# A quarter of the scan output's addition moved from VectorE to TensorE and ScalarE

## The chip, the cores and the metric

The kernel runs on one core of one Trainium2 chip. A core has five engines with an instruction queue each: TensorE (PE in the profile, with its weight loads as PEld), VectorE (DVE), ScalarE (ACT), GpSimd (POOL) and SyncE (SP, which here only issues DMAs). The metric is the device time of one execution in microseconds (us).

## The reference, cut to what matters

Two layers follow each other on an image batch of shape (8, 128, 128, 128). Layer 0 is a linear attention. Layer 1 is a state-space layer with 256 inner channels: a projection, a depthwise convolution, and then a selective scan over the 16,384 pixels of an image in four directions. The four results are added, multiplied by a gate, normalised and projected. The change is in the scan, of which this is the part that matters:

```python
def step(xc, inp):
    dlt, dut, Bt, Ct = inp
    dA = jnp.exp(dlt[..., None] * A[:, None])
    xc = dA * xc + dut[..., None] * Bt[:, :, None, :]
    y = jnp.einsum('kbcn,kbn->kbc', xc, Ct)
    return (xc, y)
...
y = (y0 + y1 + y2 + y3).transpose(0, 2, 1)
```

The state size is 1, so per pixel and channel there is one state h, the output is h times a scalar C of the pixel, and the four directions' h*C are added into one y.

## The kernel before, in words

`tile_kernel` calls `layer0`, `layer1_front` and `layer1_scan` one after the other. All that changes is in `layer1_scan`. Its work is a list of 512 **units**: 8 output images, for each of them 4 slots (one scan direction of one image each), and in each slot 16 chunks of 1,024 pixels. Channels lie on the 128 partitions, in two halves `c` = 0, 1. The running sum `y` of the output image stays in SBUF. A slot's `place` is 0 to 3 in its image. At place 0 h*C is written to `y`; at places 1, 2 and 3 (384 units) it has to be added to what `y` holds. Half of the directions see the image transposed (`y_turned`), so that their chunk lies in `y` in runs of four neighbouring elements, 512 bytes apart.

The function `step(n)` issues the instructions of one step, and `in_order` makes every engine keep exactly the order in which they are issued. A step does the end of unit n-1, the scan of unit n and the preparation of unit n+1:

- `emit(n-1, half1)`, then `gather(n-1)` and `emit(n-1, 1-half1)`. A chunk has two halves of 512 pixels. For places 1 to 3, VectorE multiplies the first half by C and writes the product to PSUM (L1001 or L1005), and `gather` (L1013, VectorE) adds it from PSUM to `y`. The other half's product stays in `ubt` (L994, VectorE), and `add` (L1021, GpSimd, at the end of the step) adds that to `y`.
- `decay(n, c)` (L960, ScalarE): the exponential, written to PSUM over the `px` pair of banks that held delta. It comes with one activation-table load.
- `weigh(n, c)` (L963, GpSimd): delta times input, in place in `ubt`.
- `scan(n, c)` (L971 or L973, VectorE): the recurrence, one instruction for 1,024 pixels.
- `delta(n+1, c)` (L952, TensorE): two matmuls of 512 columns into a `px` pair of banks, and `soften(n+1, c)` (L956, ScalarE): softplus, with another table load.
- `spread(n, half)` (L979, TensorE): the row of C copied to all partitions in PSUM (`pc`).
- loads of later units on the SP queue (L934, L935, L941), and, while an image leaves (16 steps, those at place 0 of the next image), its gate, moments, projection and store.

[...] three `px` tiles of two banks each, and two single banks. The product of the first half goes into the `px` tile of `da[n, 1]`, whose content the scan has used up. `delta(n+1, 0)` writes that same tile next, so it waits until `gather(n-1)` has read it.

Of the kernel before, what the change touches and what calls it, by code (L numbers as in the profile page):

```python
# [8 lines left out]
F32 = mybir.dt.float32  # L9
BF16 = mybir.dt.bfloat16  # L10
AF = mybir.ActivationFunctionType
ALU = mybir.AluOpType
# [4 lines left out]
P = 128  # L17
B = 8
H = W = 128
L = H * W  # L20
NH, HD = 4, 32
NC2 = 2
R = 8
K = 4
GW = 4
GN = GW * H
# [740 lines left out]
def layer1_scan(ctx: ExitStack, tc, ubs, xps, zs, gs, dtw, dtb, a_log, gamma, beta, w_out, out):  # L767
# [15 lines left out]
    nc = tc.nc  # L783
    const = ctx.enter_context(tc.tile_pool(name="l2c", bufs=1))
    big = ctx.enter_context(tc.tile_pool(name="l2b", bufs=1))
    wp = ctx.enter_context(tc.tile_pool(name="l2w", bufs=3))
    sm = ctx.enter_context(tc.tile_pool(name="l2s", bufs=4))
# [16 lines left out]
    for dst, src, rows in ((wparts, dtw.rearrange("k r d -> r k d"), R), (bparts, dtb.rearrange("o (k d) -> o k d", d=D2), 1)):  # L804
        x = wp.tile([rows, K, D2], F32, name="w32", tag="sp", bufs=2)
        nc.sync.dma_start(x, src)
        q = wp.tile([rows, 3, K, D2], BF16, name="w16", tag="ub", bufs=4)
# [14 lines left out]
    for i in range(3):  # L822
        t = const.tile([P, CH], BF16, name=f"rows{i}")
# [3 lines left out]
    for i in range(3):  # L827
        t = const.tile([P, D2], BF16, name=f"dtw{i}")
        nc.gpsimd.memset(t, 0.0)
        dws.append(t)  # L830
    csel = const.tile([P, P], BF16, name="csel")
    nc.gpsimd.memset(csel, 0.0)
    nc.gpsimd.memset(csel[96:99, :], 1.0)


    wg = const.tile([P, NC2, P], F32, name="wg")
# [4 lines left out]
    means = wp.tile([P, P], F32, name="means", tag="r", bufs=2)  # L841
    nc.vector.memset(means, 1.0 / (NC2 * P))

    mean = const.tile([P, 32], F32, name="mean2")
    nc.vector.memset(mean, 0.0)
    nc.vector.memset(mean[:, 0:1], 1.0 / (NC2 * P))
    sel = const.tile([P, NC2, 2], F32, name="sel")
    nc.vector.memset(sel, 0.0)
    for j in range(2):
# [64 lines left out]
    units = []  # L914
    for o in range(B):
        for s in ([3, 0, 1, 2] if o % 4 < 2 else [1, 2, 3, 0]):
            sl = Slot(len(units) // NCH, o, s)
            units += [(sl, i) for i in range(NCH)]

    ubt, sp, da = {}, {}, {}  # L920
# [6 lines left out]
    def load_rows(n):  # L927
        sl, i = units[n]
        m = sl.at(i)
        rw = rws[n % 3]  # L930
        md = NCH - 1 - m if sl.dt_turned_back else m
        src = xps[sl.dt_image, sl.dt_order].rearrange("j r l -> (j r) l")
        for j in range(3):
            nc.sync.dma_start(rw[3 * NR * j : 3 * NR * j + 3 * NR, :], src[:, md * CH : md * CH + CH])  # L934
        nc.sync.dma_start(rw[96:99, :], xps[sl.b, sl.order, :, R + 1, m * CH : m * CH + CH])  # L935
# [18 lines left out]
    def soften(n, c):  # L954
        sp[n, c] = t = wp.tile([P, CH], F32, name="sp", tag="sp", bufs=2)
        nc.scalar.activation(t, da[n, c], AF.Softplus)  # L956

    def decay(n, c):
        sl, i = units[n]
        nc.scalar.activation(da[n, c], sp[n, c], AF.Exp, scale=sa[:, sl.s, c : c + 1])  # L960

    def weigh(n, c):
        nc.gpsimd.tensor_tensor(ubt[n][:, c, :], ubt[n][:, c, :], sp.pop((n, c)), ALU.mult)  # L963
# [8 lines left out]
        else:  # L972
            nc.vector.tensor_tensor_scan(e, x, e, start, ALU.mult, ALU.add)  # L973

    cps, ts = {}, {}

    def spread(n, hf, tag):
        cps[n, hf] = p = pe.tile([P, 1, GN], F32, name="pc", tag=tag)
# [1 line left out]

    def emit(n, hf):

        sl, i = units[n]
        h = ubt[n][:, :, hf * 512 : hf * 512 + 512]
        c = cps.pop((n, hf)).to_broadcast([P, NC2, GN])
        if sl.place == 0:
            v = sl.y_at(i, hf)
            split = "p c (a b) -> p c a b"  # L990
            nc.vector.tensor_tensor(v, h.rearrange(split, b=H), c.rearrange(split, b=H), ALU.mult)
            return
        if hf != sl.first:
            nc.vector.tensor_tensor(h, h, c, ALU.mult)  # L994
            return
        p = da.pop((n, 1))
        if sl.y_turned:
            ts[n] = p.rearrange("p (c b a) -> p c b a", c=NC2, a=GW)
            t = p.rearrange("p (c b a) -> p c a b", c=NC2, a=GW)
            split = "p c (a b) -> p c a b"  # L1000
            nc.vector.tensor_tensor(t, h.rearrange(split, b=H), c.rearrange(split, b=H), ALU.mult)  # L1001
        else:
            t = p.rearrange("p (c q) -> p c q", c=NC2)
            ts[n] = t.rearrange("p c (a b) -> p c a b", b=H)
            nc.vector.tensor_tensor(t, h, c, ALU.mult)  # L1005

    def gather(n):

        sl, i = units[n]
        v = sl.y_at(i, sl.first)  # L1010
        if sl.y_turned:
            v = v.rearrange("p c a b -> p c b a")
        nc.vector.tensor_tensor(v, v, ts.pop(n), ALU.add)  # L1013

    def add(n):
# [8 lines left out]
    zt, rst, pts, mv = {}, {}, {}, {}  # L1024
# [8 lines left out]
    def fetch(o, m):  # L1033
        for hf in range(2):
            zt[m, hf] = z = wp.tile([P, NC2, GN], F32, name="z", bufs=6)
            p = mirrored(o, m, hf)
            nc.sync.dma_start(z, zs[o].rearrange("c p l -> p c l")[:, :, p * GN : p * GN + GN])

    def gate(o, m, hf, eng):
        z, ym = zt[m, hf], piece(m, hf)  # L1040
        eng.tensor_tensor(z, ym[:, :, ::-1] if o % 2 == 1 else ym, z, ALU.mult)

    def square(m, hf):
        nc.scalar.activation(piece(m, hf), zt[m, hf], AF.Square)  # L1044

    def moments(m):

        pm = pe.tile([P, GN], F32, name="pm", tag="pt")
        for c in range(NC2):
            for j in range(2):  # L1050
                for hf in range(2):
                    at = 32 * (2 * j + hf)
                    v = piece(m, hf) if j else zt[m, hf]
                    nc.tensor.matmul(pm[at : at + 32, :], mean, v[:, c, :], start=(c == 0), stop=(c == NC2 - 1))  # L1054
        pts[m, "rows"] = pm

    def keep(m):
        pm = pts[m, "rows"]
        pts[m, "rows"] = sr = wp.tile([P, GN], F32, name="sr", bufs=1)
        nc.scalar.copy(sr, pm)  # L1060
# [9 lines left out]
        nc.scalar.activation(t, pts[m][:, :, :, 0], AF.Square)  # L1070

    def variance(m):
        rst[m] = rstd = sm.tile([P, GW, NC2], F32, name="rstd")
        nc.vector.tensor_tensor(rstd, pts.pop(m)[:, :, :, 1], mv.pop(m), ALU.subtract)  # L1074

    def deviation(m):
        rstd = rst[m]
        nc.gpsimd.tensor_scalar(rstd, rstd, 0.0, EPS1, ALU.max, ALU.add)
        nc.gpsimd.tensor_tensor(rstd, rstd, half, ALU.pow)
# [22 lines left out]
    for o in range(B):  # L1102
        n = (o + 1) * K * NCH
        for j in range(NCH):
            e = o, NCH - 1 - j if o % 2 == 1 else j
# [11 lines left out]
    def step(n):  # L1117
        live = 0 <= n < N
        then = n + 1 < N
        before = 1 <= n <= N  # L1120
        now, last, soon, later = (leaving.get(n + i) for i in (0, -1, 1, 2))
        first = before and units[n - 1][0].place == 0
        if before:
            half1 = units[n - 1][0].first
            emit(n - 1, half1)
            if not first:
                gather(n - 1)
        if now and last:
            gate(*now, 1, nc.vector)
        if before:  # L1130
            emit(n - 1, 1 - half1)
        if n + 2 < N:
            load_rows(n + 2)
        if n in fetched:
            fetch(*fetched[n])
        if live:
            decay(n, 0)
        if now:
            square(now[1], 1)
        if live:  # L1140
            decay(n, 1)
            weigh(n, 0)
        if last:
            deviation(last[1])
        if live:
            weigh(n, 1)
        if now:
            moments(now[1])
        if live:
            scan(n, 0)  # L1150
            da.pop((n, 0))
        if last:
            for hf in range(2):
                store(*last, hf)
        if then:
            for c in range(NC2):
                delta(n + 1, c)
        if now:
            keep(now[1])
        if then:  # L1160
            soften(n + 1, 0)
        if now:
            to_tokens(now[1])
            square_mean(now[1])
        if then:
            soften(n + 1, 1)
        if live:
            scan(n, 1)
        if first:
            ubt.pop(n - 1)  # L1170
            if n + 3 < N:
                load(n + 3)
        if now:
            variance(now[1])
        if live:
            half1 = units[n][0].first
            spread(n, half1, "pc")
            spread(n, 1 - half1, "pt")
        if soon and now:
            gate(*soon, 0, nc.gpsimd)  # L1180
        elif soon:
            gate(*soon, 1, nc.gpsimd)
        elif later:
            gate(*later, 0, nc.gpsimd)
        if soon:
            square(soon[1], 0)
        if now:
            p = da.pop((n, 1)) if live else px.tile([P, CH], F32, name="px")
            for hf in range(2):
                project(now[1], hf, p[:, hf * 512 : hf * 512 + 512])  # L1190
        elif live and units[n][0].place == 0:
            da.pop((n, 1))
        if before and not first:
            add(n - 1)
            ubt.pop(n - 1)
        if n + 3 < N and not first:
            load(n + 3)
        if n in weighed:
            units[weighed[n]][0].weights()
        if n in summed:  # L1200
            add_d(*summed[n])
# [78 lines left out]
```

## Time and profile before

| what | value |
|---|---|
| median of 3 runs | 9476.79 us (9473.5 to 9477.35) |
| profiled execution: its time, its span | 9477.74 us, 9475.9 us |
| mean granted TensorE clock over the span | 0.792 |
| busy: DVE, POOL, ACT, PE, PEld | 8149.5, 7474.3, 7125.4, 6389.1, 3122.5 us |
| scans L971 and L973, 512 each | 1178.4 and 1176.9 us busy, 2332 ns each |
| `gather` L1013, 384 | 468.7 us busy, 1221 ns each |
| `add` L1021, 768 | 1155.3 us busy, 1550 ns each |

The page gives busy time per engine as a sum over three functions with different limits; the scan part fills roughly the second half of the span. A busy share close to one in a stage points at the engine that sets the time there, and the chain of waits says whether it really does.

### The profile page before, as it was taken

The page shows a single profiled execution, that of the slowest core. Times are in us where ns is not written, and L with a number is a line of the kernel's source. Part 1 is how long each engine was busy: PE and PEld are TensorE (multiplying, and loading weights), DVE is VectorE, ACT ScalarE, POOL GpSimd, SP SyncE. Part 2 cuts the span into 40 slices and gives each one's busy share as a digit, 9 for nine tenths or more (in the row PEclk, how much of TensorE's full clock was granted, in tenths as well). Part 3 has the DMA queues.
Part 4 walks back from the last instruction along what each step waited for, and adds up shares of the span by engine and source line. Part 5 has one row for each costly group of instructions (what it writes and reads, how often), then busy time and mean ns, then how long its engine had stood idle before and what let it go on. Part 6 is the DMA issues. An engine that isn't in the chain of part 4 may idle for free. (4 is left out here: it accounts for less than half of the span.)

```text
span 9475.9 us, 89695 instructions
## 1 busy us (share of the span) xinstructions
PE 6389.1 (67%) x24352; PEld 3122.5 (33%) x24352; DVE 8149.5 (86%) x8046; ACT 7125.4 (75%) x8034; POOL 7474.3 (79%) x4743
## 2 busy tenths in 40 slices
PE   8999999898989887788633644637345363543636
PEld 5555555564333332233200311304023040320403
DVE  6667765563999999999789999999999999999996
ACT  5556655567888887788678888888878888888884
POOL 3445544455789987788769999999999999999997
PEclk9999999999999998899855755758566585665857
DMA  2331233314598898999955958769586685967858
GB/s 92 134 134 71 106 134 132 133 63 152 180 230 244 231 231 229 233 232 224 226 158 171 273 154 228 223 181 264 158 238 203 190 256 166 247 187 201 248 163 214
DMA packets 1510245, 1784.08 MB, mean 188 GB/s; under 512 B 799444, under 2 KB 1025364, under 8 KB 1501552
## 3 DMA queue, kind: packets, MB, share of 16 engines
q1 hardware_dynamic: 1456496, 1577.01, 53.5%
q0 software_dynamic: 53248, 201.34, 11.4%
q8 instruction: 199, 3.26, 0.1%
q14 instruction: 302, 2.47, 0.1%
HBM read 1085.92 MB, written 692.12 MB: 188 GB/s over the span
## 5 line engine op out<-in xcount | busy, mean ns | idle before, releaser
L963 POOL TENSOR_TENSOR ubt<-ubt,sp 128x1024 f32<-128x1024 f32 x1024 | 2458.0, 2458 | 160.0 <-ACT sp L956 96.1
L952 PE MATMUL px<-rows,dtw 128*128 128x512 bf16 x2048 | 953.6, 565 | 2238.4 <-DVE y L1013 1069.2
L515 POOL TENSOR_TENSOR tap<-tap 128x1024 f32<-128x1024 f32 x512 | 1261.4, 2468 | 234.3 <-ACT tap L513 209.2
L523 DVE SCALAR_TENSOR_TENSOR acc<-xb,cw,acc 128x1024 f32<-128x1024 f32 x1024 | 1320.6, 1290 | 54.0 <-ACT xb L492 1.7
L956 ACT ACTIVATE sp<-px 128x1024 f32<-128x1024 f32 x1024 | 1046.2, 1024 | 418.1 <-PE px L952 351.0
L1021 POOL TENSOR_TENSOR y<-y,ubt 128x512 f32<-128x512 f32 x768 | 1155.3, 1550 | 146.0 <-DVE ubt L994 144.9
L505 PE MATMUL acc<-xi,wt 128*128 128x512 f32 x2048 | 1028.1, 648 | 314.3 <-ACT ures L530 314.3
L973 DVE TENSOR_TENSOR_SCAN ubt<-px,ubt 128x1024 f32<-128x1024 f32 x512 | 1176.9, 2332 | 27.4 <-POOL ubt L963 20.3
L971 DVE TENSOR_TENSOR_SCAN ubt<-px,ubt 128x1024 f32<-128x1024 f32 x512 | 1178.4, 2332 | 13.1 <-POOL ubt L963 6.0
L952 PEld LDWEIGHTS <-dtw 128*128 128x128 bf16 x2048 | 164.6, 109 | 3065.9 <-issue 869.7
L960 ACT ACTIVATE px<-sp,sa 128x1024 f32<-128x1024 f32 x1024 | 1110.1, 1109 | 6.1
L513 ACT ACTIVATE tap<-xb,cw 128x1024 f32<-128x1024 f32 x768 | 828.3, 1140 | 134.9 <-DVE acc L521 85.4
L282 POOL TENSOR_TENSOR q<-q,qs 128x512 f32<-128x512 f32 x256 | 271.7, 1061 | 698.2 <-DVE qs L281 698.2
L956 ACT ACT_TABLE_LOAD x512 | 656.9, 1283 | 169.6 <-PE px L952 146.9
L505 PEld LDWEIGHTS acc<-xi,wt 128*128 128x128 f32 x2048 | 398.1, 205 | 917.6 <-issue 497.1
L960 ACT ACT_TABLE_LOAD x512 | 656.9, 1283 | 9.0
L1086 PEld LDWEIGHTS px<-wg,z 128*128 128x128 f32 x4096 | 556.6, 219 | 117.9 <-issue 112.7
L979 PE MATMUL pc<-rows,csel 128*128 128x512 bf16 x1024 | 515.8, 584 | 81.3 <-DVE rstd L1074 77.5
L1086 PE MATMUL px<-wg,z 128*128 128x128 f32 x4096 | 556.7, 302 | 0.0
L478 PE MATMUL pxb<-xi,wi 128*128 128x512 f32 x1024 | 483.7, 595 | 10.1 <-DMA xi<-x 7.9
L1013 DVE TENSOR_TENSOR y<-y,px 128x1024 f32<-128x1024 f32 x384 | 468.7, 1221 | 14.4
L298 ACT ACTIVATE sq<-o 128x512 f32<-128x512 f32 x256 | 161.2, 630 | 420.1 <-DVE o L296 418.9
(160 smaller groups left out, 15379.7 us busy)
## 6 DMA issues: line engine op xcount, KB each, us to landing
ubt<-ubs SPq DMA_DIRECT2D x512, 1024.0 KB
zs<-z SPq DMA_DIRECT2D x512, 256.0 KB
ubs<-ures SPq DMA_DIRECT2D x256, 512.0 KB
ubs<-turned SPq DMA_DIRECT2D x256, 512.0 KB
z<-zs SPq DMA_DIRECT2D x256, 512.0 KB
y<-gs POOLq DMA_DIRECT2D x128, 1024.0 KB, 10.4
rows<-xps SPq DMA_DIRECT2D x1536, 60.0 KB
xi<-x SPq DMA_DIRECT2D x120, 576.0 KB
```

The lines of the kernel that those rows point to most:

```text
L505: nc.tensor.matmul(acc[:, s, :], wt[:, j, c, :], x, start=(j == 0), stop=(j == len(ON_PE) - 1))
L513: nc.scalar.activation(t, at(n, c, *d), AF.Copy, scale=cw[:, c, tap(*d) : tap(*d) + 1])
L515: nc.gpsimd.tensor_tensor(sums[n, c], sums[n, c], t, ALU.add)
L523: nc.vector.scalar_tensor_tensor(acc, at(n, c, *d), cw[:, c, tap(*d) : tap(*d) + 1], acc, ALU.mult, ALU.add)
L952: nc.tensor.matmul(p[:, hf * 512 : hf * 512 + 512], sl.dw[:, c * P : c * P + P], src, start=True, stop=True)
L956: nc.scalar.activation(t, da[n, c], AF.Softplus)
L960: nc.scalar.activation(da[n, c], sp[n, c], AF.Exp, scale=sa[:, sl.s, c : c + 1])
L963: nc.gpsimd.tensor_tensor(ubt[n][:, c, :], ubt[n][:, c, :], sp.pop((n, c)), ALU.mult)
L971: nc.vector.tensor_tensor_scan(e[:, ::-1], x[:, ::-1], e[:, ::-1], start, ALU.mult, ALU.add)
L973: nc.vector.tensor_tensor_scan(e, x, e, start, ALU.mult, ALU.add)
L1021: nc.gpsimd.tensor_tensor(v[:, c], v[:, c], h[:, c], ALU.add)
L1086: nc.tensor.matmul(po[:, w, :], z[:, c, w * H : w * H + H], wg[:, c, :], start=(c == 0), stop=(c == NC2 - 1))
```

## The change

The first half's product and addition are split into two quarters of a chunk. For one quarter, VectorE goes on as before: product to PSUM, `gather` adds it to `y`. For the other quarter, VectorE leaves the product in `ubt`, TensorE adds `y` and the product by multiplying both with a float32 identity matrix and accumulating in the second bank of the same `px` tile (`sum_first`, L1026), and ScalarE copies the sum to `y` (`keep_first`, L1032). "Quarter" is the half of the inner dimension, so in `y` the two quarters interleave. `emit_first` (L1013 and L1016 of the new numbering) issues the two products, `gather` is L1038, and the other half's product is L989. Two constant matrices become one column read with a stride of zero, one small buffer has three copies in place of four, and an identity of 128 x 128 is added.

```diff
-    csel = const.tile([P, P], BF16, name="csel")
+    csel = const.tile([P, 1], BF16, name="csel")
...
+    csel = csel.to_broadcast([P, P])
+    ident = const.tile([P, P], F32, name="ident2")
+    make_identity(nc, ident)
...
+    def emit_first(n):
...
+        p = da.pop((n, 1))
+        e = quarter(h, 1 - q)
+        nc.vector.tensor_tensor(e, e, quarter(c, 1 - q), ALU.mult)
+        ts[n], mine[n] = (piece_of(sl, p[:, j * GN : j * GN + GN]) for j in range(2))
+        t = ts[n].rearrange("p c b a -> p c a b") if sl.y_turned else ts[n]
+        nc.vector.tensor_tensor(t, quarter(h, q), quarter(c, q), ALU.mult)
+
+    def sum_first(n):
...
+        v = quarter(sl.y_at(i, sl.first), q)
+        xs = [contiguous(sl, x) for x in (v, quarter(hs(n, sl.first), q))]
+        for c in range(NC2):
+            for j, x in enumerate(xs):
+                nc.tensor.matmul(mine[n][:, c], ident, x[:, c], start=(j == 0), stop=(j == 1))
+
+    def keep_first(n):
...
+        v = contiguous(sl, quarter(sl.y_at(i, sl.first), q))
+        nc.scalar.copy(v, mine.pop(n))
 
     def gather(n):
 
         sl, i = units[n]
-        v = sl.y_at(i, sl.first)
-        if sl.y_turned:
-            v = v.rearrange("p c a b -> p c b a")
+        v = contiguous(sl, quarter(sl.y_at(i, sl.first), 0 if sl.back else 1))
         nc.vector.tensor_tensor(v, v, ts.pop(n), ALU.add)
...
-            emit(n - 1, half1)
-            if not first:
+            if first:
+                emit(n - 1, half1)
+            else:
+                emit_first(n - 1)
+                sum_first(n - 1)
                 gather(n - 1)
...
         if live:
             decay(n, 1)
+        if before and not first:
+            keep_first(n - 1)
+        if live:
             weigh(n, 0)
```

More of the change, by code (lines that the diff above doesn't have):

```diff
@@ L842, in layer1_scan @@
     nc.vector.memset(means, 1.0 / (NC2 * P))
-    mean = const.tile([P, 32], F32, name="mean2")
-    nc.vector.memset(mean, 0.0)
-    nc.vector.memset(mean[:, 0:1], 1.0 / (NC2 * P))
+    mean = const.tile([P, 1], F32, name="mean2")
+    nc.vector.memset(mean, 1.0 / (NC2 * P))
+    mean = mean.to_broadcast([P, 32])
     sel = const.tile([P, NC2, 2], F32, name="sel")
@@ L973, in scan @@
             nc.vector.tensor_tensor_scan(e, x, e, start, ALU.mult, ALU.add)
-    cps, ts = {}, {}
+    cps, ts, mine = {}, {}, {}
     def spread(n, hf, tag):
@@ L981, in emit @@
     def emit(n, hf):
+        h = hs(n, hf)
+        c = cps.pop((n, hf)).to_broadcast([P, NC2, GN]).rearrange("p c (a b) -> p c a b", b=H)
         sl, i = units[n]
[L986 to L992, printed above, removed]
@@ L993, in emit @@
-        if hf != sl.first:
-            nc.vector.tensor_tensor(h, h, c, ALU.mult)
-            return
-        p = da.pop((n, 1))
-        if sl.y_turned:
[L998 to L1005, printed above, removed]
+        nc.vector.tensor_tensor(sl.y_at(i, hf) if sl.place == 0 else h, h, c, ALU.mult)
@@ new lines, in hs, with quarter, contiguous, piece_of @@
+    def hs(n, hf):
+        return ubt[n][:, :, hf * 512 : hf * 512 + 512].rearrange("p c (a b) -> p c a b", b=H)
+    def quarter(v, last):
+        return v[:, :, :, H // 2 :] if last else v[:, :, :, : H // 2]
+    def contiguous(sl, v):
+        return v.rearrange("p c a b -> p c b a") if sl.y_turned else v
+    def piece_of(sl, bank):
+        if sl.y_turned:
+            return bank.rearrange("p (c b a) -> p c b a", c=NC2, a=GW)
+        return bank.rearrange("p (c a b) -> p c a b", c=NC2, a=GW)
@@ new lines, in emit_first @@
+    def emit_first(n):
+        sl, i = units[n]
+        hf, q = sl.first, 0 if sl.back else 1
+        h = hs(n, hf)
+        c = cps.pop((n, hf)).to_broadcast([P, NC2, GN]).rearrange("p c (a b) -> p c a b", b=H)
+        p = da.pop((n, 1))
+        e = quarter(h, 1 - q)
[3 more added lines that the diff above has]
+        nc.vector.tensor_tensor(t, quarter(h, q), quarter(c, q), ALU.mult)
@@ new lines, in sum_first @@
+    def sum_first(n):
+        sl, i = units[n]
+        q = 1 if sl.back else 0
+        v = quarter(sl.y_at(i, sl.first), q)
[4 more added lines that the diff above has]
+    def keep_first(n):
+        sl, i = units[n]
+        q = 1 if sl.back else 0
+        v = contiguous(sl, quarter(sl.y_at(i, sl.first), q))
+        nc.scalar.copy(v, mine.pop(n))
@@ L1007, in gather @@
     def gather(n):
         sl, i = units[n]
-        v = sl.y_at(i, sl.first)
-        if sl.y_turned:
-            v = v.rearrange("p c a b -> p c b a")
+        v = contiguous(sl, quarter(sl.y_at(i, sl.first), 0 if sl.back else 1))
         nc.vector.tensor_tensor(v, v, ts.pop(n), ALU.add)
@@ L1072, in variance @@
     def variance(m):
-        rst[m] = rstd = sm.tile([P, GW, NC2], F32, name="rstd")
+        rst[m] = rstd = sm.tile([P, GW, NC2], F32, name="rstd", bufs=3)
         nc.vector.tensor_tensor(rstd, pts.pop(m)[:, :, :, 1], mv.pop(m), ALU.subtract)
```

## Prediction

> **What bounds the kernel now.** I read the page's slices first, then the stages, then the chain and one step of the timeline. In the scan part (from slice 20 on) VectorE is at 9 tenths and TensorE's granted clock is near half. The stage view separates the two kinds of step:
>
> ```profile
> core 0: us, PE busy (x) PEld busy (x) DVE busy (x) ACT busy (x) POOL busy (x), PEclk, DMA share, GB/s
> 5294.00:5475.00 181.00, 143.47 (x986) 102.08 (x979) 170.98 (x219) 146.72 (x158) 164.94 (x89) 0.93 0.94 277
> 5481.00:5873.00 392.00, 141.16 (x298) 27.95 (x298) 383.33 (x239) 320.88 (x285) 373.57 (x201) 0.50 0.62 180
> ```
>
> The first row is 16 steps in which an image leaves, the second is steps of places 1 to 3, which the change touches. There VectorE is busy 98% of the time, GpSimd 95%, and the clock is 0.50 throughout. The chain of waits in that stretch lies on VectorE alone:
>
> ```profile
> 5602.41 1.24 DVE px L1001
> 5603.67 1.10 DVE y L1013
> 5604.81 1.01 DVE ubt L994
> 5605.82 0.12 issue
> 5605.94 4.47 DVE ubt L971 x2
> 5610.46 0.04 issue
> ```
>
> One step is product, gather, other product, two scans. The starts of those scans lie 8.22 us apart in nearly every step of places 1 to 3. Taken apart by starts: 1.26 (product, which gather needs), 1.14 (gather), 1.13 (other product), 4.69 (two scans and the way back). TensorE and ScalarE wait for VectorE:
>
> ```profile
> 5604.95 1.04 PE L952 MATMUL px<-rows,dtw 128*128 128x512 bf16 x2 [2.94 <-DVE y L1013]
> 5606.09 1.28 ACT L956 ACT_TABLE_LOAD   x1 [0.32 <-PE px L952]
> ```
>
> Delta's matmul starts 0.06 us after gather's end (5603.67 + 1.22), and 0.10 us after its own end ScalarE goes on: the two hand-over prices used below.
>
> [...] The wait priced below comes from how the program guards its buffers.
>
> **The change part by part, per step of places 1 to 3 (384 units).**
>
> *VectorE's work.* Removed: half of gather. Added: the product becomes two instructions of 512 elements. The nearest row is L272, 128x512:
>
> ```profile
> L272 DVE TENSOR_TENSOR q<-pq,qm 128x512 f32<-128x512 f32 x256 | 177.2, 692 | 26.7 <-DVE qm L270 0.9
> L551 PE MATMUL pb<-xd,ident 128*128 128x512 f32 x512 | 240.8, 593 | 0.7 <-ACT xd L543 0.7
> L1060 ACT COPY sr<-pm 128x512 f32<-128x512 f32 x128 | 75.0, 586 | 209.0 <-PE pm L1054 209.0
> ```
>
> So 0.69 us each. A follower that needs nothing of the one before starts some 0.09 us before its end (1.13 against 1.22), hence 0.60 from start to start. If nothing else happened: 0.60 (first product) + 0.73 (second, then the dependent gather) + 0.60 (gather) + 1.13 + 4.69 = 7.75 instead of 8.22: a gain of 0.47 us.
>
> *TensorE's sum.* Four matmuls of 256 columns in float32. The trace records each float32 matmul as two passes. Their price in this clock comes from L1086, passes of 128 columns:
>
> ```profile
> 5322.34 3.73 PE L1086 MATMUL px<-wg,z 128*128 128x128 f32 x32
> 5336.14 6.07 PE L1086 MATMUL px<-wg,z 128*128 128x128 f32 x32
> 5313.80:5334.10 20.30, 13.61 (x107) 9.35 (x105) 18.02 (x26) 14.87 (x16) 20.08 (x11) 1.00 1.04 292
> 5334.30:5340.90 6.60, 6.57 (x30) 6.00 (x31) 5.91 (x6) 5.55 (x7) 5.12 (x5) 0.50 1.02 350
> ```
>
> The first group ran at full clock: (3.73 - 0.17 for the last to drain) / 32 = 0.11 us a pass. The second ran 4.86 us at half clock (until 5341.0) and 1.21 us at full. The fast part holds (1.21 - 0.17) / 0.11 = 9 passes, so 23 took 4.86 us: 0.21 each. A 256-column pass is then 0.22 us at full and 0.43 us at half clock, and the eight passes of the sum are 1.7 or 3.4 us, plus a drain of 0.2. That the stationary matrix is an identity makes it no cheaper: L551 multiplies with one and takes 593 ns for 512 columns at mostly full clock, as other float32 rows do (L1054: 628). Weight loads, 0.2 us in L505's and L1086's rows, lie beside such passes.
>
> *Where the sum lies.* This decides. In the changed kernel's built order, the first identity matmul waits for VectorE's **second** product (same `px` tile, though another bank), and in all 384 units gather waits for the **last** identity matmul. Gather writes one quarter of `y` while TensorE reads the other; they interleave, and the program guards the whole range. So the sum stands between second product and gather on the engine that bounds the step, and the other product and both scans queue behind gather. Nothing hides it. Per step at half clock:
>
> 0.60 (first product) + 0.69 (second, to its end) + 0.06 + 3.41 + 0.21 + 0.08 (hand-overs, sum, drain) + 0.60 (gather) + 1.13 + 4.69 = 11.47 us, **3.25 us more** than 8.22. At full clock 9.77, 1.55 more.
>
> *Which clock.* TensorE's step becomes 3.4 (sum) + 0.85 (delta 0), a pause, 0.85 + 0.86 (delta 1, spread), a pause. [...] I take 3.2.
>
> *ScalarE's copy.* 586 ns by L1060. It waits for gather and then for nothing: `decay(n, 1)` ends 3.4 us into the step, gather after 5.7. Delta 0, its table load and softplus stand behind it. After gather: copy 0.65, delta 0 1.1, table load 1.28, softplus 1.02, second softplus after scan 0's delta 1 (10.3 to 11.3), table load, exponentials done by 3.4 us into the next step, whose first scan starts at 6.8. Covered by the stalled VectorE. If the stall were gone it would not be: then decay 1, copy 0.53, delta 0 with hand-overs 1.2, table 1.28, two softplus 1.97, table 1.3, two exponentials 2.16 form a ring of 8.5 us, longer than 8.22.
>
> *GpSimd.* 7.9 us of work per step, starting later, still within 11.4. *DMA.* As many issues as before; loads of `ubt` also wait for TensorE's reads, done well before. *The constants and the buffer.* `csel` and `mean` as one column: same weight loads, TensorE has spare time there; the identity is built once. Nothing.
>
> *Sum.* 384 x 3.2 = 1,229 us on the profiled execution's 9477.74 gives 10,707; the median is 1 us lower. I round down to **10,700**, since in the steps at an image's end, 9.5 to 10.2 us long, a little of the stall may lie beside other waits.
>
> *Unknown.* In transposed slots the product is read by TensorE in steps of 512 bytes. [...] Here a ScalarE copy read that way (L617) took 1988 ns against 1007 (L487), 1.9 ns an element. At half clock a pass takes 1.7 ns a column anyway, so the least is nothing and my value is nothing; the most, twice the time for four of eight passes, is 1.7 us in 192 steps, 330 us. [...]
>
> **The rivals.**
> - *Fast clock.* If the longer sum lifts the clock for good, the step is 9.77: 384 x 1.55 = 595, some 10,070; half of the steps give 10,380. For it: the stages with an image leaving run at 0.93. Against it: the pauses above. 0.10.
> - *Strided reads at full price*: 11,030. 0.10.
> - *The wait costs nothing at run time*, as if the sum were done when gather comes. Then the ring over ScalarE decides: (8.5 - 8.22) x 384 = 107, about 9,585. 0.05.
> - *Faster.* The sum leaves VectorE's path and the fast clock takes 0.4 us off delta 0 in the ring (8.1). Then GpSimd at 7.95 or that ring bound the step, and 0.1 to 0.27 x 384 gives 9,375 to 9,440. It needs sum and hand-overs under 0.47 us of VectorE's time against 3.8 priced. 0.03.
> - *Nothing in effect*, sums cancelling: 0.02, within 0.2%, which is about what a measurement of this kernel can tell from no change.
> - The main case: 0.70, own range 10,550 to 10,850.
>
> **How the numbers follow.** The forecast is the main case. The range 10,370 to 10,930 takes in its errors, the nearer half of the fast-clock case and most of the strided one. Chances: faster 0.03, same 0.02, slower 0.95.
>
> **What would show it.** Gather's idle time before it, released by PE L1026, of 3.5 us or more per step; VectorE's share in these stretches down from 98% to about 70%; scan starts 11.4 us apart; L1026 eight passes of 0.43; clock mostly 0.5 with single fast windows. I am wrong if gather follows the second product at once, if the clock stays at 1 through the sum, or if transposed slots have longer steps than the others by over 0.3 us.

## The result and the profile after

The changed kernel takes 10644.99 us (median of 6 runs, 10636.52 to 10652.03) against 9476.14 us before (median of 6): a ratio of 1.1235, 95% interval 1.1221 to 1.125. It is slower by 1,169 us; the forecast was 10,700, with a range of 10,370 to 10,930. The profiled execution of the changed kernel took 10636.52 us, 1,158.8 more than the profiled one of before.

VectorE's busy tenths and the granted clock in 40 slices, from the page of the kernel before and then from that of the changed kernel:

```profile
DVE  6667765563999999999789999999999999999996
PEclk9999999999999998899855755758566585665857
...
DVE  6666655739999999977687686786776866867765
PEclk9999999999999889975686685675766856867768
```

In the right half, the stage of the scans, VectorE now stands at 6 to 8 tenths, where it was at 9 almost throughout, and the clock moves mostly between 0.5 and 0.8. The group of gather before, then those of gather, of the sum's matmuls and of the copy in the changed kernel (engine, tiles, count, busy us, mean ns, then the idle time just before them and who ended it):

```profile
L1013 DVE TENSOR_TENSOR y<-y,px 128x1024 f32<-128x1024 f32 x384 | 468.7, 1221 | 14.4
...
L1038 DVE TENSOR_TENSOR y<-y,px 128x512 f32<-128x512 f32 x384 | 264.1, 688 | 1368.8 <-PE px L1026 1368.8
...
L1026 PE MATMUL px<-y,ident 128*128 128x256 f32 x1536 | 787.5, 611 | 528.0 <-DVE px L1016 528.0
...
L1026 PE MATMUL px<-ubt,ident 128*128 128x256 f32 x1536 | 764.3, 591 | 0.0
...
L1032 ACT COPY y<-px 128x512 f32<-128x512 f32 x384 | 224.1, 584 | 513.3 <-DVE y L1038 513.3
```

VectorE sat idle before gather for 1368.8 us, and all of it ended with TensorE's sum: 3.56 us for each of 384 gathers, where before it was 14.4 us in all. VectorE's busy time fell from 8149.5 to 7960.6 us, 0.49 us for each gather. The two together, 1,354 - 189 = 1,165 us, are the loss within 7 us.

The chain of waits in one step of place 1 (start, us, what):

```profile
5695.85 0.69 DVE ubt L1013
5696.54 0.62 DVE px L1016
5697.15 0.04 issue
5697.20 3.80 PE px L1026 x8
...
5701.02 0.07 DVE y L1038
...
5701.62 1.22 DVE ubt L989
5702.84 4.51 DVE ubt L974 x2
...
5707.45 0.69 DVE ubt L1013
```

Where gather stood in the chain before with 1.10 us, there are now 3.80 us of TensorE's sum, and then 0.62 us until the other product starts (5701.00 to 5701.62), in which the shorter gather lies. The step is 11.60 us (5695.85 to 5707.45), where it was 8.22.

By place, the mean from scan start to scan start, taken from the traces (images 2 to 8), with all such steps of the kernel summed:

| place | before, us | after, us | all steps, before and after, us |
|---|---|---|---|
| 0 | 11.22 | 11.05 | 1371, 1351 |
| 1 | 8.36 | 11.71 | 1067, 1497 |
| 2 | 8.22 | 11.42 | 1052, 1462 |
| 3 | 8.31 | 10.93 | 1056, 1387 |

Places 1 to 3 give 430 + 410 + 331 = 1,171, place 0 gives back 20, and the first scan starts 7 us later: within 2 us the 1,158.8 of the profiled executions. That place 3 loses less is the clock, below.

### The profile page after: what moved, and what is told of

Same layout as the page of the kernel before. It is cut to its first block, busy times and chain, and to the rows that moved or that the text cites. A ratio compares the mean times of both kernels' runs of the same rounds, so it can differ in the third digit from the quotient of the medians.

```text
span 10634.7 us, 97031 instructions
## 1 busy us (share of the span) xinstructions
PE 7607.5 (72%) x27424; PEld 4006.0 (38%) x27424; DVE 7960.6 (75%) x8429; ACT 7320.6 (69%) x8418; POOL 7468.7 (70%) x4745
## 4 chain that ended last, share of the span: by engine, by line
DVE 21%; ACT 13%; PE 11%; DMA 4%; issue 4%; SPq 0%; DVEq 0%; ACTq 0%; POOL 0%
DVE ubt L974 7%; DVE ubt L976 7%; PE px L1026 6%; ACT px L963 4%; DVE ubt L989 4%; ACT sp L959 3%; ACT L963 3%; PE px L955 2%; DMA out<-r 2%; DVE r L1117 2%; ACT L959 2%; PE px L1111 2%; DVE ubt L1013 1%; DVE px L1016 1%; DMA ubt<-ubs 1%
## 5 line engine op out<-in xcount | busy, mean ns | idle before, releaser
L966 POOL TENSOR_TENSOR ubt<-ubt,sp 128x1024 f32<-128x1024 f32 x1024 | 2411.4, 2372 | 649.4 <-ACT sp L959 576.3
L955 PE MATMUL px<-rows,dtw 128*128 128x512 bf16 x2048 | 870.3, 543 | 1666.6 <-DVE ubt L976 675.6
L1038 DVE TENSOR_TENSOR y<-y,px 128x512 f32<-128x512 f32 x384 | 264.1, 688 | 1368.8 <-PE px L1026 1368.8
L1026 PE MATMUL px<-y,ident 128*128 128x256 f32 x1536 | 787.5, 611 | 528.0 <-DVE px L1016 528.0
L959 ACT ACTIVATE sp<-px 128x1024 f32<-128x1024 f32 x1024 | 1023.4, 1023 | 123.2 <-POOL y L1046 63.3
L955 PEld LDWEIGHTS <-dtw 128*128 128x128 bf16 x2048 | 209.9, 116 | 2283.2 <-issue 1118.1
L1026 PE MATMUL px<-ubt,ident 128*128 128x256 f32 x1536 | 764.3, 591 | 0.0
L1026 PEld LDWEIGHTS px<-y,ident 128*128 128x128 f32 x1536 | 399.8, 288 | 956.6 <-DVE px L1016 814.8
L1032 ACT COPY y<-px 128x512 f32<-128x512 f32 x384 | 224.1, 584 | 513.3 <-DVE y L1038 513.3
```

The costliest lines, as they stand in the source:

```text
L955: nc.tensor.matmul(p[:, hf * 512 : hf * 512 + 512], sl.dw[:, c * P : c * P + P], src, start=True, stop=True)
L1026: nc.tensor.matmul(mine[n][:, c], ident, x[:, c], start=(j == 0), stop=(j == 1))
```

## The experiments

The theory after the result: VectorE's step waits for TensorE's sum, and the clock sets how long. The rivals: the copy on ScalarE with all that stands behind it, or the added work itself wherever VectorE stands. A "ring" in the expectations is a chain of waits that comes back to the same instruction one or two steps later, and so sets the least time of a step. All lines of code are changes to the changed kernel, and times stand against its 10,645 us and against about 9,470 of the kernel before. half_sum, no_copy, gather_first and delta_twice are one execution each; vector_only and late_sum are medians of 4, own_bank of 9.

**half_sum: half of the sum.**

```diff
-        for c in range(NC2):
+        for c in range(1):
             for j, x in enumerate(xs):
                 nc.tensor.matmul(mine[n][:, c], ident, x[:, c], start=(j == 0), stop=(j == 1))
```

> The changed kernel, but TensorE sums only channel half c = 0 of the quarter (four passes in place of eight); for c = 1 the sum is left out, so that quarter of y is not valid. Theory (gather waits for TensorE's sum, and VectorE's whole step waits behind it): the stall before gather falls from 3.57 us on average by four passes, some 1.7 us at half clock, less where the clock is already fast: steps of places 1 to 3 of 9.6 to 10.0 us and a total of 9,980 to 10,120 us. Rival (the time goes to ScalarE's copy and what stands behind it, or to the hand-overs between engines, whatever the size of the sum): over 10,450 us.

Measured: 10097.38 us; steps of 9.9 to 10.0 us. Its gather and sum, from the groups:

```profile
L1026 PE MATMUL px<-y,ident 128*128 128x256 f32 x768 | 443.2, 678 | 398.5 <-DVE px L1016 398.5
L1038 DVE TENSOR_TENSOR y<-y,px 128x512 f32<-128x512 f32 x384 | 264.2, 688 | 802.6 <-PE px L1026 786.6
```

The wait for TensorE fell to 786.6 us, by 582, and the time by 548. With half of the sum about half of the loss of 1,169 us went, although the copy and every hand-over were still there: it is the size of the sum that costs.

**no_copy: without ScalarE's copy.**

```diff
-        nc.scalar.copy(v, mine.pop(n))
+        mine.pop(n)
```

> The changed kernel without ScalarE's copy of the sum back to y (384 copies of 584 ns left out, so that quarter of y stays as it was). Theory: the copy lies beside VectorE's stall, so steps stay at 11.4 to 11.7 us at half clock; total 10,530 to 10,780 us, the width for how the TensorE clock falls when delta starts 0.65 us earlier. Rival (copy, delta, table load and softplus behind it set the step): the step loses 0.6 us or more, under 10,420 us.

Measured: 10766.18 us, within the theory's width. Nothing is gained by taking the copy away, so it lay beside the stall; the typical step is 11.59 to 11.67 us, where it was 11.60. The kernel even became slower by 121 us, and the clock accounts for it: the wait before gather grew by 125 to 1493.8 us, and the mean clock fell from 0.813 to 0.788. The reason is in the section on what was right and wrong.

**vector_only: VectorE's part of the change alone.**

```diff
-                sum_first(n - 1)
...
-            keep_first(n - 1)
+            mine.pop(n - 1)
```

> The changed kernel without TensorE's sum and without ScalarE's copy; VectorE's instructions are all there, the other quarter is left out of y. Theory: VectorE needs 7.75 us a step by the sum in the prediction, and GpSimd with 7.9 us of work sets the pace: 7.9 to 8.1 us, total 9,370 to 9,430 us, against about 9,476 before. Rival (splitting the product in two costs VectorE more than half a gather saves): 9,480 us or more.

Measured: 9320.45 us, a ratio to before of 0.984 (0.9823 to 0.9856). That is faster than the theory said. One step of its timeline and the start of the next (start, us, engine, line, what), and then its stage view (us, busy and count of PE, PEld, DVE, ACT and POOL, granted clock, DMA share, GB/s):

```profile
5561.44 4.68 POOL L966 TENSOR_TENSOR ubt<-ubt,sp 128x1024 f32<-128x1024 f32 x2
...
5562.47 0.69 DVE L1013 TENSOR_TENSOR ubt<-ubt,pc 128x512 f32<-128x512 f32 x1
5563.07 0.69 DVE L1016 TENSOR_TENSOR px<-ubt,pc 128x512 f32<-128x512 f32 x1
5563.80 0.69 DVE L1038 TENSOR_TENSOR y<-y,px 128x512 f32<-128x512 f32 x1
5564.40 1.22 DVE L989 TENSOR_TENSOR ubt<-ubt,pc 128x1024 f32<-128x1024 f32 x1
5565.53 4.58 DVE L974 TENSOR_TENSOR_SCAN ubt<-px,ubt 128x1024 f32<-128x1024 f32 x2
...
5566.06 3.21 POOL L1046 TENSOR_TENSOR y<-y,ubt 128x512 f32<-128x512 f32 x2
...
5569.22 4.66 POOL L966 TENSOR_TENSOR ubt<-ubt,sp 128x1024 f32<-128x1024 f32 x2
...
5570.22 0.69 DVE L1013 TENSOR_TENSOR ubt<-ubt,pc 128x512 f32<-128x512 f32 x1
...
5500.00:5850.00 350.00, 137.57 (x335) 32.65 (x335) 338.89 (x273) 301.02 (x271) 349.46 (x189) 0.52 0.68 196
```

The step is 7.75 us (5562.47 to 5570.22), to the hundredth the prediction's sum for VectorE. GpSimd keeps up only just: it is busy 349.46 of these 350 us, and its own step, from product to product, takes 7.78 us (5561.44 to 5569.22), a little more than VectorE's. It lives off a lead: in image 2, its product was done 1.9 us ahead of the scan early in place 1 and 1.3 us at the end of place 2. At the end of place 3, where it has gates to compute as well, the lead is used up. By the groups the scans waited 47.4 us for GpSimd's product over the whole kernel, against 26.3 before. 384 x 0.47 = 180 us is what VectorE's part can bring at most; 151 came, and these 21 us are most of the rest. The changed constants and the smaller buffer are in this kernel too, and cost nothing that shows.

**gather_first: gather issued before the sum.**

```diff
-                sum_first(n - 1)
                 gather(n - 1)
+                sum_first(n - 1)
```

> The changed kernel with two lines exchanged: gather is issued before the sum, so VectorE's gather no longer waits for TensorE; the sum waits for gather instead. All work is as before the exchange. Theory (the time is the wait of VectorE for the sum): VectorE goes on at once, and what is left is a ring over two steps: gather, sum 3.8, copy 0.65, delta 1.1, table load and two softplus 3.4, table load and exponential 2.4, two scans 4.7, products and gather 2.0, some 18.2 us for two steps at half clock and 16 at full: steps of 8.4 to 9.2 us, total 9,550 to 9,870 us. Rival (TensorE's and ScalarE's added work itself costs the time, wherever VectorE stands): over 10,300 us.

Measured: 9806.77 us, with every instruction of the changed kernel still in it. VectorE no longer waits for the sum (13.6 us before all gathers); its waits stand elsewhere and are shorter. Its two rows of scans, and one round of the chain of waits in place 2:

```profile
L974 DVE TENSOR_TENSOR_SCAN ubt<-px,ubt 128x1024 f32<-128x1024 f32 x512 | 1179.9, 2335 | 246.8 <-POOL ubt L966 237.4 <-ACT px L963 5.0 <-issue 3.7
L976 DVE TENSOR_TENSOR_SCAN ubt<-px,ubt 128x1024 f32<-128x1024 f32 x512 | 1178.4, 2334 | 257.3 <-POOL ubt L966 249.2 <-ACT px L963 3.8 <-issue 3.2
...
5645.03 2.36 DVE ubt L974
...
5647.44 0.62 PE px L955 x2
...
5649.44 1.03 ACT sp L959
...
5650.54 2.38 POOL ubt L966
...
5653.90 2.36 DVE ubt L974
```

The scans wait for GpSimd's product, which waits for softplus (L966 after L959, 561.5 us), which waits for delta (605.4 us). In 372 of the 384 steps delta 0 in turn waits for the step's own first scan, whose `px` tile it takes over. So the ring closes within one step, and neither sum nor copy lies on it. It is not the ring over two steps of the expectation; that the two are about equally long (8.9 to 9.3 us a step here, 18.2 for two there) is chance, and so is the time inside its range. What the run was made for stands: exchanging two lines took off 838 us of the 1,169, so the loss is a matter of who waits.

**own_bank: the sum in another bank.** VectorE's second product and gather keep the `px` tile; the sum goes into the single bank of C.

```diff
-        ts[n], mine[n] = (piece_of(sl, p[:, j * GN : j * GN + GN]) for j in range(2))
+        ts[n] = piece_of(sl, p[:, :GN])
...
         sl, i = units[n]
+        bank = pe.tile([P, 1, GN], F32, name="mine", tag="pc")
+        mine[n] = piece_of(sl, bank[:, 0])
```

> The changed kernel with one thing moved: TensorE's sum goes to the single bank that held C of the first half (free once the second product has read it), not to the second bank of the px tile that gather reads. The quarters still interleave in y. In the built order gather then waits for the second product alone, and delta 0 waits for gather, not for ScalarE's copy. Theory (the wait came with the shared px tile): VectorE's stall goes; what is left is VectorE's 7.75 us of work, or a ring over two steps (second product, sum 3.8, delta 1.0, table load and softplus 3.4, table load and exponential 2.4, two scans 4.7, products 1.3: 16.5 us at half clock, 14.3 at full). Steps of 7.75 to 8.3 us, total 9,320 to 9,500 us. Rival (the interleaved quarters of y make the wait, as the prediction said): no change, over 10,500 us.

Measured: 9447.34 us, ratio to before 0.9977 (0.9967 to 0.9987). Gather's row is now

```profile
L1040 DVE TENSOR_TENSOR y<-y,px 128x512 f32<-128x512 f32 x384 | 263.8, 687 | 13.7
```

with 13.7 us of idle time in all. The quarters of `y` interleave as before, so it was not `y`: the wait came because sum and product lay in one `px` tile. Its steps take 8.1 to 8.3 us on average, as the ring would have it that the expectation priced at 16.5 us for two. In one stretch the chain of waits does run from sum to sum over two steps, by delta, softplus, GpSimd's product, scan and products:

```profile
5499.28 3.76 PE mine L1028 x8
...
5506.39 2.38 POOL ubt L966
...
5515.88 3.76 PE mine L1028 x8
```

That is 16.60 us. In other stretches it takes other ways, so that this ring sets all steps is not shown.

**late_sum: the sum between the deltas.** As own_bank, with the bank of the other half's C, and the sum and copy moved to where less stands behind them.

```diff
-                sum_first(n - 1)
                 gather(n - 1)
...
+        late = then and not now
+        if before and not first and not late:
+            sum_first(n - 1)
...
         if then:
-            for c in range(NC2):
-                delta(n + 1, c)
+            delta(n + 1, 0)
+        if before and not first and late:
+            sum_first(n - 1)
+        if then:
+            delta(n + 1, 1)
...
+        if before and not first and late:
+            keep_first(n - 1)
         if then:
             soften(n + 1, 1)
```

> As own_bank, but the sum goes to the single bank of the other half's C, is issued on TensorE between delta 0 and delta 1, and ScalarE copies it between the two softplus (in the steps in which an image leaves, in the old place). Delta 0 and its softplus no longer stand behind the sum, but the sum starts only after the other half's product, and delta 1, its softplus and the next spread of C stand behind sum and copy. Theory: VectorE's 7.75 us where the clock is fast, 8.3 to 8.5 where it is slow; total 9,320 to 9,560 us. Rival (whatever place TensorE gets it in, the sum costs a full stall): over 10,300 us.

Measured: 9385.38 us, ratio to before 0.9911 (0.9896 to 0.9926). It does all the work of the changed kernel and takes less time than either, 0.9% less than the kernel before. Against vector_only, which leaves sum and copy out, the two now cost 65 us in place of 1,325. Its stage view over places 1 to 3, beside that of the changed kernel:

```profile
5470.00:5830.00 360.00, 235.90 (x633) 126.76 (x631) 346.71 (x272) 330.44 (x319) 355.35 (x191) 0.78 0.64 187
```

```profile
5640.00:6160.00 520.00, 282.21 (x644) 137.38 (x644) 350.08 (x276) 332.43 (x322) 362.18 (x195) 0.64 0.46 132
```

VectorE is busy 96% of the time in late_sum and 67% in the changed kernel. GpSimd is busy 99% in late_sum, so that with its work as it is little more can be gained.

**delta_twice: more work for TensorE.**

```diff
-            nc.tensor.matmul(p[:, hf * 512 : hf * 512 + 512], sl.dw[:, c * P : c * P + P], src, start=True, stop=True)
+            for _ in range(2):
+                nc.tensor.matmul(p[:, hf * 512 : hf * 512 + 512], sl.dw[:, c * P : c * P + P], src, start=True, stop=True)
```

> The changed kernel with every delta matmul issued twice, so 0.85 us more of TensorE work for each delta at half clock, at times when VectorE waits for nothing of it. Theory (the stall is the sum at the clock that TensorE's business earns): [...] more sums run at full clock (1.99 in place of 3.78 us), and the kernel with more work is faster: 10,000 to 10,550 us. Rival (TensorE's time is the load, or deltas are on the path): slower than the changed kernel, 10,700 us or more.

Measured: 10613.11 us in one run, missing both expectations. The rival is out: it asked for 10,700 us or more, and twice the delta work did not slow the kernel. The theory's direction held: by the trace 144 sums ran at full clock in place of 81, and the wait before gather fell from 1368.8 to 1313.0 us. But only 48 of them lie in place 3, where a fast sum saves 1.79 us; the changed kernel had 51 there. The others lie in transposed slots and save 0.91. Place 0's steps took 41 us more (1,392 against 1,351), which I did not look into. Nor is it a clean test of the clock: delta 0 now waits for the copy in 357 of 384 steps, in place 3 too, where in the changed kernel it waits for the scan, so the matmuls lie in other blocks. The change against the changed kernel, 0.3%, is too small for one run to prove.

## Why the prediction was right, and where not

- **VectorE's work, -0.47 us a step.** Right: vector_only's step is 7.75 us. The 512-element products and gather took 687 to 690 ns, as the row it was priced by (692).
- **The sum lies between second product and gather, nothing hides it.** Right, and it carries the result: the wait is released by TensorE in all 384 gathers, it shrinks with the sum (half_sum), and it goes with the wait (gather_first, own_bank).
- **Why gather waits: "Gather writes one quarter of `y` while TensorE reads the other; they interleave, and the program guards the whole range."** Wrong. own_bank leaves the interleaving and loses the wait. It was the shared `px` tile, which the prediction had named only for the wait ahead of the sum. The price was not touched by it, but the repair is: another tile, not another cut of `y`.
- **The sum's size, 3.41 + 0.21.** Slightly short: at half clock it took 3.78 us from first start to last end, since the second pass started 0.59 us after the first and not 0.43. The typical step is 11.60 us instead of 11.47.
- **Which clock: 3.2 us a step, 0.05 under the price at half clock.** The term that was mis-sized; the 0.05 was the author's estimate. By the trace 81 of 384 sums ran at full clock, 30 in place 2 and 51 in place 3: 30 x 0.91 + 51 x 1.79 = 118 us, 0.31 a step. The prediction had delta 0 alone after the copy, then a pause. So it is in place 1. But in 88 of 128 steps of place 2 and 119 of place 3, the trace has delta 0 waiting for the scan, with delta 1 right behind it, since the copy is long done by then. Both deltas and the spread of C then run in one block. TensorE's timeline of the changed kernel in place 3 (start, duration, line, what, and in brackets the wait before it):

```profile
6069.90 1.89 PE L955 MATMUL px<-rows,dtw 128*128 128x512 bf16 x4 [4.17 <-DVE ubt L974]
6071.58 1.06 PE L982 MATMUL pc<-rows,csel 128*128 128x512 bf16 x2
6073.60 0.70 PE L1026 MATMUL px<-y,ident 128*128 128x256 f32 x2 [0.96 <-DVE px L1016]
6074.14 0.59 PE L1026 MATMUL px<-ubt,ident 128*128 128x256 f32 x2
```

The same stretch of the changed kernel by windows (columns as in the stage view above, the granted clock ahead of the DMA share):

```profile
6069.50:6072.80 3.30, 2.74 (x6) 0.73 (x6) 3.13 (x3) 1.75 (x2) 0.71 (x1) 0.50 0.05 11
6073.00:6076.20 3.20, 1.99 (x8) 1.44 (x8) 1.11 (x2) 3.17 (x4) 2.77 (x2) 1.00 0.90 251
6076.40:6079.60 3.20, 0.00 (x0) 0.00 (x0) 3.20 (x2) 1.85 (x3) 3.20 (x3) 1.00 0.31 115
```

The trace has the clock change at 6069.44, 6072.86 and 6079.68: to half, to full and to half again. The block fills 2.74 of the 3.42 us at half clock, 80%; the sum falls into the 6.82 us at full clock and takes 2.0 us. In no_copy delta 0 waits for gather again and runs apart from delta 1; no sum there lay wholly at full clock, which fits its 121 us. So the two errors, 0.13 x 384 = 50 us too little for the sum and 0.26 x 384 = 100 too much for the clock, leave 50 us; the forecast stood 55 above the median. That the number came so close is in part luck: the two errors have opposite signs, and the 20 us that place 0 gave back stand against the forecast's rounding down (7 us) and the 7 us of the later start.
- **ScalarE's copy costs nothing.** Right (no_copy).
- **Strided reads, nothing at half clock, on 192 units.** The price was right: at half clock a sum takes 3.78 us in transposed slots and in the others. The count was not: places 1 and 2 are the transposed ones, 256 units. At full clock the stride does show: 2.88 us against 1.99. A pair of passes over the product at full clock, first in place 2 and then in place 3:

```profile
5906.70 1.04 PE L1026 MATMUL px<-ubt,ident 128*128 128x256 f32 x2
...
6075.00 0.59 PE L1026 MATMUL px<-ubt,ident 128*128 128x256 f32 x2
```

- **GpSimd's 7.9 us a step as the next bound.** Right in kind, a little too long: in vector_only GpSimd, hardly ever idle, takes 7.78 us a step, just above VectorE's 7.75. The forecast did not rest on it; the faster rival did.

What stays open: why the tile that delta 0 gets changes between places in the changed kernel. The traces show that it does, and that it differs between the runs; I did not trace the cause in the pool.

## What to carry to other kernels

Work moved off the bounding engine helps only if that engine doesn't wait for it: look first at which buffer the helper's result and the bounding engine's own next operand share, because the waits here followed the tile and not the bank (1368.8 us before gather with the sum in the other bank of its `px` tile, 13.7 in own_bank). Price a TensorE helper at the clock of its stage, float32 passes included, and then put it where its consumers are furthest away. The same sum and copy cost 1,325 us in one tile and place and 65 us in another.

## What the runs showed of the hardware

- In the changed kernel a float32 matmul of 256 columns against a 128x128 identity took two passes of 0.43 us each at half clock and 0.22 at full, no less per column than the weights of L1086 in the kernel before (128 columns: 0.21 and 0.11 us).
- In the changed kernel a pass of 256 columns over a moving operand with a stride of 512 bytes took 0.45 us at half clock, against 0.43 without it, and 0.42 us at full clock, against 0.22.
- In the changed kernel, after deltas and spread had filled 2.74 of 3.42 us at half clock (6069.44 to 6072.86), the sum behind them ran at full clock and took 1.99 us in place of 3.78. With every delta issued twice, 144 of 384 sums ran at full clock, where it had been 81.
